# Early convolution of the first image: taps shared by two routes in every chunk, and the second pass's first weights placed over dead weights

## The chip, the cores and the metric

The kernel runs on one core of one Trainium2 chip. The time is device microseconds (us) of that core for one execution of the whole program; lower is better. All arithmetic is float32. The engines are TensorE (PE, with its weight loads as PEld), VectorE (DVE), ScalarE (ACT), GpSimd (POOL) and SyncE (SP), which here only issues DMAs. Each engine takes its instructions in the order in which the program lists them.

## What is computed

Two layers run one after the other on `x` of shape (8, 32, 32, 512): 8 images of 1024 pixels with 512 channels. The reference, cut to what matters:

```python
# layer 0: group norm, self-attention with 8 heads of 64 channels, residual
x_norm = group_norm(x, gn_scale, gn_bias)                    # 32 groups
q, k, v = split(x_norm @ w_qkv + b_qkv)
out = softmax(q k^T / 8) v                                   # per image and head, 1024 x 1024
x = x + out @ w_out + b_out

# layer 1: deformable attention
x_ln = layernorm(x, ln_g, ln_b).transpose(0, 3, 1, 2)
x_flat = x_ln.reshape(b, c, h * w).reshape(b, h * w, c)      # a reshape, not a transpose back
q = x_flat @ wq + bq
o = depthwise_conv(q.reshape(b, c, h, w), dw_w, 7x7, stride 2, padding 3)   # 16 x 16 points
offsets = conv1x1(gelu(o + dw_b), pw_w)                      # 2 numbers per point
grid = reference_points + tanh(offsets)
s = bilinear_sample(x, grid)                                 # 256 sampled rows of 512
v = k = s @ wv + bv
qh, kh, vh = heads(q @ mq_w + mq_b), heads(k @ mk_w + mk_b), heads(v @ mv_w + mv_b)
z = softmax(qh kh^T) vh @ mo_w + mo_b + x                    # 1024 queries, 256 keys
out = gelu(layernorm(z) @ mlp_w + mlp_b) + z
```

Each output of the depthwise convolution is a sum of 49 products, one for each place (u, v) of the 7x7 window. One such product and sum over a whole block of 128 channels and 256 points is called a *tap* below.

## The kernel before

**Two passes.** Pass 1 (lines 386 to 773) computes layer 0 for all images, pass 2 (lines 776 to 1195) layer 1 for all images. Between them lie two tensors in DRAM for each image: `mid`, the output of layer 0, and `hat_d`, its layer norm with scale and shift. The 512 channels are handled as four chunks of 128 partitions. The place where pass 1 ends and pass 2 begins is called the *seam*.

**Units of pass 1.** A unit is one tile of 128 queries of one pair of heads in one image. There are 32 units an image, 256 in all; where the text counts units of the last image it counts 0 to 31, and 32 and up are places after the last unit. `MovedAttention.push` writes one unit: TensorE computes the scores `sc<-k,q` (two heads, 128x1024 each), VectorE takes the row maxima `nmax`, ScalarE the exponentials `e`, and VectorE transposes them in blocks of 32x32 into `sq`. After every second unit 16 DMAs on SP move the blocks into `et`, the exponentials with keys on the partitions. Two to four units later TensorE multiplies `et` by the values (`av<-et,v`). After four units the eight sums are inverted and spread (`rs`, `rep`), turned on TensorE and copied (`inv`), and VectorE scales the result into `attT`. When an image is done, `out_steps` (lines 558 to 603) multiplies `attT` by `wout`, adds the residual tile `xr` with the bias row `bout` (which GpSimd has added to `xr` before), stores `mid`, takes the layer norm's statistics (`stats`, `mv`; GpSimd raises to the power -1/2), normalizes into `hat`, multiplies and adds the rows `lng_row` and `lnb_row` on GpSimd, and stores `hat_d`.

**The order of the work.** Whatever a unit does beside its own scores is put on a list as `at(place, step)` with a place in units, and `run_due(until)` (lines 345 to 353) writes out, in order of place, all steps due. `InOrder` keeps the written order on every engine. So a place decides the order on each engine's queue, and no scheduler changes it. A step that needs TensorE for another unit's work (the products `q`, `k` and `v` of the next pair of heads, for example, at the places in `pair_places` and, for the last pair, in `last_pair`) is called a *filler* below.

**The tail of pass 1.** For the last image the projection by `wout` comes after its last unit, at the places of `last_places` (lines 622 to 628): tiles 0 to 3, which need only the first half of the queries, from place 33.1 on, and tiles 4 to 7 from place 36 on. Its `mid` stores are issued on ScalarE's queue, its `hat_d` stores on GpSimd's; in the images before, both are on SP's.

**The early convolution** (`first_conv`, lines 630 to 715). The convolution of image 0 in pass 2 needs only `hat_d` of image 0, which is there long before. So it is computed in pass 1, among the units of the last image, by chunks of output channels 0 to 3. `fetch` loads `wq` into four buffers, its bias row, and the tap weights `dww_x`. For each chunk `operand` loads two halves of `hat_d`, `fill` multiplies them by `wq` on TensorE (two matmul groups), and `fill_end` adds the bias row and writes the result into an image with a border of zeros, the *pad* (`conv_pad`). Then come 49 taps, in one of two forms (`conv_tap`):

- alone: one VectorE instruction multiplies the strided pad by the tap weight and adds it to the accumulator;
- shared: ScalarE writes the product into one half of a small buffer `part_x` (two halves, used in turn), and GpSimd adds it to the accumulator.

All 49 taps of chunks 0 and 1 are shared; they use one pad, which lies with the bias row in a buffer of the tag `xT`. All 98 taps of chunks 2 and 3 are alone; their two pads and their accumulators lie in a tile of the tag `wqkv`, 24,576 bytes on each partition, which takes the place of the layer's `w_qkv` weights and so can be filled only when the last product with these is done. Of the 98, ten are placed from unit 27.9 on, sixteen with the eight `wout` tiles (two for each), and 72 after all tiles. `store` sends the finished sums to `o_first` in DRAM by GpSimd's queue.

**The start of pass 2** (`prep`, lines 836 to 873). SP's queue issues `wq_r` (the weight `wq` again), `wv`, `mk_w`, seven small vectors, and later `mv_w` and `mq_w`. TensorE turns `wq_r` and `wv` (16 transposes each), and then multiplies them by `mk_w`, `mv_w` and `mq_w` (`product`, four groups each), so that later each of keys, values and queries takes one product. `add_cols` makes the bias columns. `points(0)` (lines 943 to 951) stands after the first of the four `mq_w` products: it loads `o_first` (as `o`, on SP), applies gelu on ScalarE, computes the offsets on TensorE (`mm<-pww,o`), tanh, the corner indices on VectorE, gathers rows of `mid` with indirect DMAs on GpSimd's queue, and sums them with their weights into `smp`. After `prep` come the four key steps and two value steps of image 0 and the first units of pass 2. Small loads for the convolution (`load_conv`: `dwb`, `dww`, two for `pww`) and the rows `bq_row`, `bo_row`, `bm_row` are issued in `load_late`, behind the `mv_w` bias column.

**Pools of pass 2** (line 783). A pool's buffers take the addresses that pass 1 leaves, in the order in which the pools are opened, and a load into a buffer waits until all that lay at its addresses in pass 1 has been read. Here the order is

```python
cv, late, late2, first, cvhat, raw, wp
```

where `first` holds `wq_r`, `raw` the raw weights `wv`, `mk_w`, `mv_w`, `mq_w` in two buffers of 8,192 bytes a partition, and `cv` the small tiles of the convolution and two pads.

Of the kernel before, what the change touches and what calls it, by code (L numbers as in the profile page):

```python
# [9 lines left out]
F32 = mybir.dt.float32  # L10
# [220 lines left out]
def attention_then_deformable_attention(  # L231
# [137 lines left out]
    def conv_tap(acc, pad, dww, cb, u, v, part=None):  # L369

        tap = dww[:, cb, u * KS + v : u * KS + v + 1]
        src = pad[:, ds(u, G, 2), ds(v, G, 2)]
        acc = acc.rearrange("p (i j) -> p i j", j=G)
        first = u == 0 and v == 0
# [11 lines left out]
    with ExitStack() as l0:  # L386
# [171 lines left out]
        def out_steps(b, attT, places, last=False):  # L558
# [22 lines left out]
            def summed(t):  # L581
# [3 lines left out]
                stats = work.tile([P, 6], F32, tag="stats", name="stats1", bufs=2)  # L585
# [44 lines left out]
        def first_conv(n):  # L630
# [3 lines left out]
            room = {"pad": {}, "o": {}}  # L634

            def fetch():
# [3 lines left out]
                rest = work.tile([P, NC, QB], F32, tag="xT", name="rest_x", bufs=NX_T)  # L640
                rest = rest.rearrange("p c q -> p (c q)")
                room["bq"] = rest[:, 0:C]
# [3 lines left out]
                pad = rest[:, ds(C, PADH * PADW)]  # L646
                nc.gpsimd.memset(pad, 0.0)
                pad = pad.rearrange("p (i j) -> p i j", j=PADW)
                part = work.tile([P, C], F32, tag="hat", name="part_x", bufs=3)
                o = work.tile([P, C], F32, tag="hat", name="o_x", bufs=3)  # L650
                room["part"] = part
                for cb in range(2):
                    room["pad"][cb], room["o"][cb] = pad, o[:, ts(cb, NS)]

            def fetch2():
                pads = wp.tile([P, NC, 3 * C], F32, tag="wqkv", name="pads_x")
                o = pads[:, 2, :]
                for i in range(2):
                    pad = pads[:, i, 0 : PADH * PADW]
                    nc.gpsimd.memset(pad, 0.0)  # L660
                    room["pad"][2 + i] = pad.rearrange("p (i j) -> p i j", j=PADW)
                    room["o"][2 + i] = o[:, ts(i, NS)]
# [16 lines left out]
            def fill_end(cb, par):  # L679
                conv_pad(room["pad"][cb], room["ps", cb, par], room["bq"], par)  # L680

            def tap(cb, i, part):
                conv_tap(
                    room["o"][cb], room["pad"][cb], room["dww"], cb, i // KS, i % KS,
                    (lambda: room["part"][:, ts(i % 2, NS)]) if part else None,
                )

            def store(cb):
                nc.gpsimd.dma_start(o_first[:, cb, :], room["o"][cb])

            at(n + 10.5, fetch)
            at(n + 24, fetch2)
            taps = KS * KS
            for cb, start in enumerate((12.2, 22.5, 25.2, 27.2)):
                at(n + start - 1.6, lambda cb=cb: operand(cb))
                for par in range(2):
                    at(n + start + par, lambda cb=cb, par=par: fill(cb, par))
                    at(n + start + par + 0.65, lambda cb=cb, par=par: fill_end(cb, par))
                if cb < 2:
                    for i in range(taps):  # L700
                        at(n + start + 1.7 + 0.18 * i, lambda cb=cb, i=i: tap(cb, i, True))
                    at(n + start + 10.7, lambda cb=cb: store(cb))


            for j in range(2 * taps):
                cb, i = divmod(j, taps)
                if j < 10:
                    place = n + 27.9 + 0.4 * j
                elif j < 26:
                    place = last_places(n + per, (j - 10) // 2)[2] + 0.02  # L710
                else:
                    place = n + per + 12
                at(place, lambda cb=cb + 2, i=i: tap(cb, i, False))
# [515 lines left out]
```

## Time and profile before

| | us |
|---|---|
| three timed runs | 3788.79, 3792.98, 3794.7 (median 3792.98) |
| the profiled execution's own time | 3789.67 |
| span of that execution on the core | 3788.0 |
| TensorE busy | 3578.3 (94%) |
| VectorE busy | 2789.1 (74%) |
| ScalarE busy | 1529.3 (40%) |
| GpSimd busy | 750.6 (20%) |

Every time of a trace is in microseconds from the start of the span. The mean granted clock of TensorE over the span is 0.975 of full speed. The seam lies near 2070 us: pass 1 takes some 55% of the span. Nearly all instructions are recorded by one helper, so all carry one line number (L53), and groups are told apart by their tiles: `mm<-wout,attT` is a matmul that reads `wout` and `attT` and writes a tile `mm`; a trailing `_x` marks tiles of the early convolution, and numbers of buffers are left out. In the rows, `PE mm L53 <- DMA wq_r: 9.0, 1, 9.0` says that TensorE stood idle before an `mm` instruction 9.0 us in all, in one wait, longest 9.0, and that what ended the wait was the landing of the load of `wq_r`; `x16 [9.01 <-...]` in a timeline is a group of 16 instructions and the idle time before it. `SPq` is the issuing queue of SP.

### The profile page before, as it was taken

Reading aid. Unit: us, or ns where it says so; the run is one execution under the profiler, and the core shown is the slowest. Engines: PE = TensorE matmul, PEld = TensorE weight load, DVE = VectorE, ACT = ScalarE, POOL = GpSimd, SP = SyncE. Lnnn points to the kernel's source line nnn. Section 1 sums busy time; section 2 is a strip of 40 time slices with the busy share of each in tenths; the row PEclk is TensorE's granted clock in tenths of the full one; section 3 lists DMA queues with packets and bytes.
Section 4 is the critical chain, followed back from the end, with each engine's and each line's share of the span. In section 5 each row is a group of like instructions: output and inputs, shape, how many; then the busy total and the mean of one; then the engine's idle time right before and its main releaser. Section 6 shows DMA issues by size and latency. Waiting matters only on the chain.

```text
span 3788.0 us, 46075 instructions
## 1 busy us (share of the span) xinstructions
PE 3578.3 (94%) x16152; PEld 1868.9 (49%) x16152; DVE 2789.1 (74%) x4264; ACT 1529.3 (40%) x3218; POOL 750.6 (20%) x838
## 2 busy tenths in 40 slices
PE   8999999999999999999998787999999999999997
PEld 4554554545545455455453434454545454544543
DVE  5678777776777777867766569898988888888333
ACT  3443443433434434344364123343434343444443
POOL 0003012020030120301346201121121212121212
PEclk9999999999999999999999898999999999999999
DMA  5667666665666666655755501021111111110100
GB/s 154 155 158 188 164 168 170 162 184 153 162 189 159 170 168 163 188 155 150 199 143 143 176 1 67 34 71 41 67 45 56 56 56 56 56 56 34 59 23 31
DMA packets 235350, 438.23 MB, mean 116 GB/s; under 512 B 49296, under 2 KB 53392, under 8 KB 232176
## 3 DMA queue, kind: packets, MB, share of 16 engines
q1 hardware_dynamic: 212528, 363.08, 35.4%
q0 software_dynamic: 21440, 70.11, 5.8%
q8 instruction: 129, 2.11, 0.2%
q10 hardware_dynamic: 1152, 2.10, 0.2%
q14 instruction: 101, 0.83, 0.1%
HBM read 115.84 MB, written 50.86 MB: 44 GB/s over the span
## 4 chain that ended last, share of the span: by engine, by line
PE 69%; DVE 20%; issue 6%; DMA 1%; ACT 1%; POOL 1%; SPq 0%; DVEq 0%; POOLq 0%; ACTq 0%
PE mm L53 42%; PE sc L53 15%; PE av L53 13%; DVE o L53 10%; DVE nmax L53 3%; DVE stats L53 1%; DVE sq L53 1%; DVE pad L53 1%; POOL mv L53 1%; ACT e L53 1%; DVE z L53 1%; DVE zn L53 1%; DVE attH L53 1%; DVE mv L53 1%; DMA row<-mid,ii 0%
## 5 line engine op out<-in xcount | busy, mean ns | idle before, releaser
L53 ACT ACTIVATE e<-sc,nmax 128x1024 f32<-128x1024 f32 (+1 forms) x1024 | 804.6, 799 | 901.8 <-DVE nmax L53 901.3
L53 DVE TENSOR_REDUCE nmax<-sc 128x1 f32<-128x1024 f32 (+1 forms) x640 | 753.2, 1219 | 481.5 <-PE sc L53 480.3
L53 DVE SCALAR_TENSOR_TENSOR o<-pad,dww,o 128x256 f32<-128x256 f32 x1344 | 721.3, 537 | 44.1
L53 DVE STREAM_TRANSPOSE sq<-e 128x1024 f32<-128x1024 f32 x512 | 608.1, 1226 | 50.8 <-ACT e L53 49.5
L53 PE MATMUL sc<-k,q 64*128 64x512 f32 x2048 | 527.3, 618 | 13.5 <-ACT q L53 6.2
L53 PE MATMUL av<-et,v 128*64 128x256 f32 x4096 | 504.2, 389 | 16.3 <-DMA et<-sq 9.4
L53 PE MATMUL mm<-xT,wqkv 128*128 128x512 f32 x1024 | 471.5, 604 | 2.6 <-issue 2.6
L53 PEld LDWEIGHTS av<-et,v 128*64 128x64 f32 x4096 | 276.0, 138 | 322.9 <-issue 177.2
L53 POOL TENSOR_TENSOR mv<-mv,minus_half 128x1 f32<-128x1 f32 x128 | 74.3, 581 | 1396.3 <-DVE mv L53 1334.1
L53 PEld LDWEIGHTS sc<-k,q 64*128 64x128 f32 x2048 | 181.6, 186 | 276.2 <-issue 229.8
L53 PEld LDWEIGHTS mm<-xT,wqkv 128*128 128x128 f32 x1024 | 185.9, 191 | 226.8 <-issue 219.7
L53 ACT COPY et<-mm 128x512 f32<-128x512 f32 x256 | 140.7, 593 | 317.6 <-PE mm L53 317.4
L53 PE MATMUL mm<-wqkv,xT 128*128 128x128 f32 x2048 | 244.5, 278 | 0.0
L53 PEld LDWEIGHTS mm<-wqkv,xT 128*128 128x128 f32 x2048 | 233.8, 192 | 19.9 <-issue 19.9
L53 PE MATMUL mm<-wm,zT 128*128 128x512 f32 x512 | 240.4, 613 | 2.9 <-ACT zT L53 2.9
L53 PE MATMUL mm<-hat_h,wqq 128*128 128x512 f32 x512 | 236.7, 605 | 0.0
L53 PE MATMUL mm<-wo,attH 128*128 128x512 f32 x512 | 231.4, 595 | 3.1 <-DVE attH L53 3.1
L53 PE MATMUL mm<-wout,attT 128*128 128x512 f32 x512 | 233.7, 601 | 0.0
L53 ACT ACTIVATION_READ_ACCUMULATOR e<-sc,nmax 128x1 f32 x1024 | 209.2, 204 | 0.0
L53 PE MATMUL mm<-wq_r,hat 128*128 128x512 f32 x448 | 203.8, 598 | 0.2 <-ACT et L53 0.2
L53 PE MATMUL mm<-ident,e 128*128 128x128 f32 x1024 | 152.6, 293 | 26.7 <-DVE z L53 11.4
L53 PEld LDWEIGHTS mm<-hat_h,wqq 128*128 128x128 f32 x512 | 92.1, 189 | 143.0 <-issue 131.6
(153 smaller groups left out, 3629.5 us busy)
## 6 DMA issues: line engine op xcount, KB each, us to landing
et<-sq SPq DMA_DIRECT2D x2048, 128.0 KB, 2.7
xr<-in_x_dram POOLq DMA_DIRECT2D x64, 256.0 KB, 3.7
hat_h<-hat_d SPq DMA_DIRECT2D x16, 1024.0 KB, 5.3
xr<-mid SPq DMA_DIRECT2D x64, 256.0 KB, 3.1
out_dram<-res POOLq DMA_DIRECT2D x64, 256.0 KB, 2.3
x<-in_x_dram POOLq DMA_DIRECT2D x60, 256.0 KB, 3.8
mid<-xr SPq DMA_DIRECT2D x56, 256.0 KB, 2.9
hat_d<-hat SPq DMA_DIRECT2D x56, 256.0 KB, 2.9
```

The source lines that it names most:

```text
L53: return self.tc.keep_in_program_order(op(*args, **kwargs))
```

## The change

It has three parts.

1. *The taps of every chunk are split between the two routes.* `conv_tap` takes a running tap number and a flag for the first of an accumulator. Taps 0 to `shared[cb]`-1 of chunk `cb` are shared (29, 29, 29, 11), the rest alone (20, 20, 20, 38), into the second half of the chunk's `o_x` buffer; `store` adds the two halves on VectorE before the DMA. The pads come from two buffers of the tag `xT` instead of the tile over `w_qkv` (chunks 0, 1 and 3 use the one, chunk 2 the other), the accumulators from the tags `hat` and `x`. The fills move to the places in `fills`, the taps start at `begins` with a shared tap every 0.18 and an alone tap every 0.265 units. Chunk 3's first 24 taps of both kinds come with the `wout` tiles, three for each, and the last 14 alone after all of them. `last_pair` moves four of the last pair's six fillers: 21.3 to 22.3, 22.3 to 23.3, 23.3 to 24.3 and 23.6 to 25.3. The tail's `stats` get a tag of their own.
2. *Another order of pools in pass 2.* `wq_r` and the two raw-weight buffers come first and so lie where `w_qkv` lay, 24,576 bytes a partition; the two pads and the rows `bo_row` and `bm_row` get a pool `padp` of their own.
3. *Two moves in* `prep`. `load_conv` goes from `load_late` to the place before the load of `mv_w`, and `points(0)` from after the first `mq_w` product to after the second `mk_w` product, six groups and two bias columns earlier.

```diff
@@ -366,12 +366,12 @@
         )
-    def conv_tap(acc, pad, dww, cb, u, v, part=None):
-
+    def conv_tap(acc, pad, dww, cb, i, first, part=None):
+
+        u, v = divmod(i, KS)
         tap = dww[:, cb, u * KS + v : u * KS + v + 1]
...
         acc = acc.rearrange("p (i j) -> p i j", j=G)
-        first = u == 0 and v == 0
         if part is not None:
@@ -582,7 +582,7 @@
                 to_mid.dma_start(dst[:, t, :], xr)
-                stats = work.tile([P, 6], F32, tag="stats", name="stats1", bufs=2)
+                stats = work.tile([P, 6], F32, tag="stats1", name="stats1", bufs=2)
                 mv = room["mv", t] = work.tile([P, 3], F32, tag="mv1", name="mv1", bufs=3)
@@ -631,35 +631,25 @@
-            room = {"pad": {}, "o": {}}
+            room = {}
             def fetch():
...
                     nc.gpsimd.dma_start(room["w"][c], by_chunk(wq)[:, c, :])
-                rest = work.tile([P, NC, QB], F32, tag="xT", name="rest_x", bufs=NX_T)
-                rest = rest.rearrange("p c q -> p (c q)")
-                room["bq"] = rest[:, 0:C]
+                rest = padded(0)
+                room["bq"] = rest[:, ds(PADH * PADW, C)]
                 nc.gpsimd.dma_start(room["bq"], bq.partition_broadcast(P))
...
                 nc.gpsimd.dma_start(room["dww"], dw_w.rearrange("(c p) a u v -> p c (a u v)", p=P))
-                pad = rest[:, ds(C, PADH * PADW)]
+
+            def padded(i):
+                rest = work.tile([P, NC, QB], F32, tag="xT", name="rest_x", bufs=NX_T)
+                rest = rest.rearrange("p c q -> p (c q)")
+                pad = rest[:, 0 : PADH * PADW]
                 nc.gpsimd.memset(pad, 0.0)
-                pad = pad.rearrange("p (i j) -> p i j", j=PADW)
-                part = work.tile([P, C], F32, tag="hat", name="part_x", bufs=3)
-                o = work.tile([P, C], F32, tag="hat", name="o_x", bufs=3)
-                room["part"] = part
-                for cb in range(2):
-                    room["pad"][cb], room["o"][cb] = pad, o[:, ts(cb, NS)]
-
-            def fetch2():
-                pads = wp.tile([P, NC, 3 * C], F32, tag="wqkv", name="pads_x")
-                o = pads[:, 2, :]
-                for i in range(2):
-                    pad = pads[:, i, 0 : PADH * PADW]
-                    nc.gpsimd.memset(pad, 0.0)
-                    room["pad"][2 + i] = pad.rearrange("p (i j) -> p i j", j=PADW)
-                    room["o"][2 + i] = o[:, ts(i, NS)]
+                room["pad", i] = pad.rearrange("p (i j) -> p i j", j=PADW)
+                return rest
             def operand(cb):
@@ -677,42 +667,44 @@
             def fill_end(cb, par):
-                conv_pad(room["pad"][cb], room["ps", cb, par], room["bq"], par)
-
-            def tap(cb, i, part):
+                conv_pad(room["pad", pad_of[cb]], room["ps", cb, par], room["bq"], par)
+
+            def tap(cb, i, alone):
+                if i == 0:
+                    tag = dict(tag="hat", bufs=3) if cb < NC - 1 else dict(tag="x", bufs=NX)
+                    room["o", cb] = work.tile([P, C], F32, name="o_x", **tag)
+                    if cb in (0, NC - 1):
+                        room["part"] = work.tile([P, C], F32, name="part_x", **tag)
                 conv_tap(
-                    room["o"][cb], room["pad"][cb], room["dww"], cb, i // KS, i % KS,
-                    (lambda: room["part"][:, ts(i % 2, NS)]) if part else None,
+                    room["o", cb][:, ts(int(alone), NS)], room["pad", pad_of[cb]], room["dww"], cb, i,
+                    i in (0, shared[cb]), None if alone else lambda: room["part"][:, ts(i % 2, NS)],
                 )
             def store(cb):
-                nc.gpsimd.dma_start(o_first[:, cb, :], room["o"][cb])
-
+                o = room["o", cb]
+                nc.vector.tensor_tensor(o[:, 0:NS], o[:, 0:NS], o[:, ts(1, NS)], ALU.add)
+                nc.gpsimd.dma_start(o_first[:, cb, :], o[:, 0:NS])
+
+            pad_of = (0, 0, 1, 0)
+            shared = (29, 29, 29, 11)
+            fills = ((12.35, 13.35), (20.6, 21.3), (26.3, 27.3), (28.3, 29.3))
+            begins = (14.05, 22.05, 28.0, 33.05)
             at(n + 10.5, fetch)
-            at(n + 24, fetch2)
-            taps = KS * KS
-            for cb, start in enumerate((12.2, 22.5, 25.2, 27.2)):
-                at(n + start - 1.6, lambda cb=cb: operand(cb))
+            at(n + 22.4, lambda: padded(1))
+            for cb in range(NC):
+                at(n + fills[cb][0] - 1.6, lambda cb=cb: operand(cb))
                 for par in range(2):
-                    at(n + start + par, lambda cb=cb, par=par: fill(cb, par))
-                    at(n + start + par + 0.65, lambda cb=cb, par=par: fill_end(cb, par))
-                if cb < 2:
-                    for i in range(taps):
-                        at(n + start + 1.7 + 0.18 * i, lambda cb=cb, i=i: tap(cb, i, True))
-                    at(n + start + 10.7, lambda cb=cb: store(cb))
-
-
-            for j in range(2 * taps):
-                cb, i = divmod(j, taps)
-                if j < 10:
-                    place = n + 27.9 + 0.4 * j
-                elif j < 26:
-                    place = last_places(n + per, (j - 10) // 2)[2] + 0.02
-                else:
-                    place = n + per + 12
-                at(place, lambda cb=cb + 2, i=i: tap(cb, i, False))
-            at(n + per + 13, lambda: store(2))
-            at(n + per + 13, lambda: store(3))
+                    at(n + fills[cb][par], lambda cb=cb, par=par: fill(cb, par))
+                    at(n + int(fills[cb][par]) + 0.95, lambda cb=cb, par=par: fill_end(cb, par))
+                for i in range(KS * KS):
+                    alone, j = i >= shared[cb], i - shared[cb] * (i >= shared[cb])
+                    place = n + begins[cb] + (0.265 if alone else 0.18) * j
+                    if cb == NC - 1:
+
+                        place = last_places(n + per, j // 3 % NT)[2] + 0.02
+                        place = place if j < 24 else n + per + 12
+                    at(place, lambda cb=cb, i=i, alone=alone: tap(cb, i, alone))
+                at(n + begins[cb] + (5.1 if cb < NC - 1 else 20), lambda cb=cb: store(cb))
         per = NHP * NT
@@ -725,7 +717,7 @@
         ]
-        last_pair = (19.3, 20.3, 21.3, 22.3, 23.3, 23.6)
+        last_pair = (19.3, 20.3, 22.3, 23.3, 24.3, 25.3)
         norm_places = [
@@ -780,8 +772,8 @@
             return l1.enter_context(tc.tile_pool(name=name, bufs=bufs, reuse_waits="tile"))
-        cv, late, late2, first, cvhat, raw, wp = (
-            pool(n) for n in ("cv", "late", "late2", "first", "cvhat", "raw", "w2")
+        first, raw, padp, cv, late, cvhat, late2, wp = (
+            pool(n) for n in ("first", "raw", "padp", "cv", "late", "cvhat", "late2", "w2")
         )
@@ -826,7 +818,7 @@
         nc.vector.tensor_scalar(refs, refs, -1.0, None, ALU.add)
-        pads = [cv.tile([P, PADH, PADW], F32, tag=f"pad{i}", name=f"pad{i}") for i in range(PADS)]
+        pads = [padp.tile([P, PADH, PADW], F32, tag=f"pad{i}", name=f"pad{i}") for i in range(PADS)]
         for pad in pads:
@@ -854,6 +846,7 @@
             load_small()
+            load_conv()
             for m in range(NC):
@@ -864,7 +857,7 @@
                     product(dst, k, raws[name], i)
-                    if name == "mq" and i == 0:
+                    if name == "mk" and i == 1:
                         points(0)
@@ -895,7 +888,7 @@
                 conv_out(b)
-            conv_tap(room[b, "o"][:, cb, :], pads[cb % PADS], dww, cb, i // KS, i % KS)
+            conv_tap(room[b, "o"][:, cb, :], pads[cb % PADS], dww, cb, i, i == 0)
         def conv_gelu(b):
@@ -1157,9 +1150,8 @@
             wm = load_w(late2, mlp_w, "wm")
-            bo_row = load_row(late, mo_b, "bo_row")
-            bm_row = load_row(late2, mlp_b, "bm_row")
-            load_conv()
+            bo_row = load_row(padp, mo_b, "bo_row")
+            bm_row = load_row(padp, mlp_b, "bm_row")
         def rows():
...
```

## The prediction

> **What bounds the kernel now.** I read the page first: whole-span shares, then the chain. TensorE is busy 94% and carries 69% of the chain, so only places where TensorE waits, or does nothing useful, can pay.
>
> ```profile
> PE 3578.3 (94%) x16152; PEld 1868.9 (49%) x16152; DVE 2789.1 (74%) x4264; ACT 1529.3 (40%) x3218; POOL 750.6 (20%) x838
> ...
> PE 69%; DVE 20%; issue 6%; DMA 1%; ACT 1%; POOL 1%; SPq 0%; DVEq 0%; POOLq 0%; ACTq 0%
> ```
>
> The change lies around the seam of the two passes, so next the waits of TensorE from 2030 to 2200 us (in all, times, longest), and TensorE's timeline there (start, us, group, count, idle before it and what ended that).
>
> ```profile
> PE av L53 <- DMA et<-sq: 9.4, 1, 9.4
> PE mm L53 <- DMA wq_r<-in_L_conv_wq_dram: 9.0, 1, 9.0
> PE mm L53 <- DVE smp L53: 8.8, 1, 8.8
> PE mm L53 <- ACT o L53: 2.5, 1, 2.5
> ```
>
> ```profile
> 2062.26 6.59 PE L53 MATMUL av<-et,v 128*64 128x256 f32 x32 [9.40 <-DMA et<-sq]
> 2070.47 13.90 PE L53 MATMUL mm<-wout,attT 128*128 128x512 f32 x32
> 2093.38 3.65 PE L53 MATMUL mm<-ident,wq_r 128*128 128x128 f32 x16 [9.01 <-DMA wq_r<-in_L_conv_wq_dram]
> 2143.01 3.55 PE L53 MATMUL mm<-pww,o 128*128 128x2 f32 x16 [2.50 <-ACT o L53]
> 2181.24 7.03 PE L53 MATMUL mm<-wvv,smp 128*128 128x512 f32 x16
> ```
>
> Four holes, 29.7 us. The second ends on a weight load, the third on the gather of `points(0)`; those two, 17.8 us, are what the change goes for. The start of the value steps, 2181.24, is my finish line: from there the second pass is the same in both programs, and VectorE, which bounds its first images, is idle 23.64 us up to 2195.23, so a shift there moves all that follows.
>
> Then who sets the seam. These are rows of GpSimd's timeline, of VectorE's, and two waits of SP's queue:
>
> ```profile
> 2039.75 3.23 POOL L53 DMA_DIRECT2D xr<-in_x_dram  x6
> 2047.88 5.30 POOL L53 TENSOR_TENSOR xr<-xr,bout 128x512 f32<-128x512 f32 x4 [1.46 <-DMA xr<-in_x_dram]
> 2053.14 3.92 POOL L53 TENSOR_TENSOR o_x<-part_x,o_x 128x256 f32<-128x256 f32 x5
> ```
>
> ```profile
> 2092.09 15.01 DVE L53 SCALAR_TENSOR_TENSOR pads_x<-pads_x,dww_x 128x256 f32<-128x256 f32 x23
> 2107.40 24.96 DVE L53 SCALAR_TENSOR_TENSOR pads_x<-pads_x,dww_x 128x256 f32<-128x256 f32 x48
> ```
>
> ```profile
> SPq L53 <- DVE mv L53: 27.8, 1, 27.8
> SPq L53 <- DMA mid<-xr: 15.0, 1, 15.0
> ```
>
> GpSimd's queue is the hidden bound: the last `et` pieces stand on SP behind the first two `mid` stores (15.0), those stand on ScalarE behind taps that wait for GpSimd's adds, and these stand behind the six `xr` adds. VectorE's 72 late taps end at 2132.4, which is why `points` cannot come sooner.
>
> Last, busy time in single units (PE, PEld, DVE, ACT, POOL): the cover for new taps.
>
> ```profile
> 1914.81:1922.23 7.42, 7.42 (x33) 3.18 (x32) 4.73 (x4) 5.20 (x10) 3.82 (x6) 1.00 0.30 78
> 2006.68:2014.10 7.42, 7.42 (x33) 3.18 (x32) 6.57 (x8) 5.48 (x11) 4.47 (x7) 1.00 0.72 180
> ```
>
> **Part by part.** *Taps in the units.* Chunks 0 to 2 now put 20 taps each on VectorE, at 3 or 4 a unit. A tap repeats every 0.52 us (24.96/48). Units 22 to 29 then hold on VectorE 8 x 4.73, 28 taps 14.6, four pads at 0.69, two `rs`/`rep` pairs at 1.07, two `attT` at 0.65, one new sum near 0.4: 59.0 us, against TensorE's 60.4 (7.42 a unit, 7.56 with values, 7.82 with `rep`). Units 14 to 19: 42.7 against 45.6. `nmax` may come some 2.0 us late before the next scores wait (5.4 us of other matmuls, less 1.2 of `nmax`, 2.2 of exponentials). So it fits, barely: cost 0, cover 1.4 + 2.0 us. A tap beside GpSimd's adds: below, 0.485 alone; above, 0.83, the longest beside such an add; three there average 0.60 (0.51, 0.47, 0.83), which I take as the nearest: same tap, same adds. Cover over 28 taps is 0.12 each: it holds to 0.64 from tap to tap, and 0.60 with the gap is 0.635.
> [...]
>
> *Matmuls moved.* Nothing is added on TensorE; fillers go from units 22 and 23 into 24 and 29. Unit 24 was empty (0.73 idle and 1.2 of waits inside its scores): -1.95. But `k` now ends right before unit 24's scores: +0.8, as `sc<-k,q` waited 0.78 for `q` in unit 15. The sums at units 19 and 27 wait for GpSimd's last add and hold `sq`: 2.5 us, hidden by `et` slack of about 2.5, +0.3. So unit 30's scores start at 2017.1 (2017.9 less 0.85). Then VectorE has no hole: scores 1.9, lag 0.7, `nmax` 2.4, four taps with `sq`, `rs` and `rep` 5.2, `nmax` 2.4, an exponential 1.2: `inv` at 2030.9 instead of 2033.88. Six adds follow in 5.9, as before: GpSimd's `xr` loads begin at 2036.8, 3.0 sooner. Its loads and adds take 13.4 (2039.75 to 2053.14): 2050.2.
>
> *The tail of pass 1.* Now worse. GpSimd has 6 adds instead of 5 (0.78 each) before the sum of chunk 2, and VectorE's sum stands ahead of `xr` of tile 0, which stood free before. From 2050.2: adds 4.7, sum 0.4, `xr` 0.7, statistics 1.1, 3 taps 1.4, `xr` of tile 1 0.7: its `mid` store goes out at 2059.2 (before about 2056.2), so the last `et` lands near 2065, +3. Behind it GpSimd carries 8 of chunk 3's adds between the tiles' `mv` and `hat`. From 2050.2: 14 adds 11.0, four `mv` 2.4, two `hat` pairs 5.3, three stores 2.5, waits for VectorE 2.5: 23.7; VectorE's last `hat`, `rs` and `rep` 2.2: 2076.1, against 2069.98: +6.1. The same wout follows: TensorE done at 2090.5 (before 2084.4).
>
> *Weights.* `wq_r`, `wv`, `mk` wait only for the last pieces of `et` and a `mid` store, near 2072: landing in 5.7 to 11.9 they are there by 2084. The 9.0 us hole goes; next late is the third transpose, for `xr` of tile 7 (about 2094). Six more groups 5.1, a copy 0.6, two products 6.9: TensorE is at `points` near 2107.
>
> *Points earlier.* GpSimd's chain ends 54.7 after 2050.2 (before 44.7 after 2053.14; eleven more adds, 8.6, and 1.4 of waits). VectorE's last 14 taps start at 2097.8; six squeeze in beside it, 8 run free, 4.2: 2108.2; sum 0.4, store 2.2 (2132.66 to 2134.86), `o` load: 3.6 as before, or 9.2 if the 1 MB `mv` load now just ahead (5.6) delays it fully; I take 4.2. Table 1.28, first gelu 0.43, offsets 3.55: 2120.3. So TensorE waits about 10 us here, where it waited 2.5: what the weight load gave is half given back. SP's four small convolution loads now stand ahead of `mv` and `o`, and the first of them waits for the last taps: `mv` goes out near 2109 instead of 2101.5, needed at 2131; `mq` behind `o` and mk's end, lands at 2137, needed at 2148: hidden by 17 us of products, and a late one would cost its lateness one for one.
>
> *Rest.* Two mk products 6.9, three bias columns 3.5 each, eight products 27.6: 45.0. The granted clock was 0.55 to 0.69 for some 10 us after holes like this (2090 to 2100, 2160 to 2170): a cost between 0 and 5, I take 2.5. TensorE reaches the key steps at 2167.8; the gather, 21.6 us (2150.0 to 2171.6), is done near 2146, so no hole. Key steps 4 x 1.81 at full clock: value steps at 2175.0 against 2181.24.
>
> **The sum:** -6.2 us. The profiled execution took 3789.67 (span 3788.0, 1.7 around it): 3783.5. It stands 3.3 under the median of the three, 3792.98; for the median I say 3787.
>
> **Rivals.**
> *The convolution is there in time.* Every microsecond that GpSimd's tail is shorter is one gained, up to the 10 that TensorE waits. For it: `xr` landed in 7.0 us, 3.8 is its median elsewhere (-3); the clock's 2.5; my GpSimd waits of 2 may vanish. 3776 to 3784, say 3780. Against it: GpSimd's order holds eleven more adds, whatever their luck.
> *Slower: VectorE and GpSimd in each other's way.* Place: units 14 to 29 and the tail's taps. At 0.86 a tap (0.83 and the gap) instead of 0.52, units 22 to 29 overrun their cover by 6.2 us and 14 to 19 by 1.8, which takes the 6.2 back and 1.8 more; in the tail, where taps beside 1.26 us operations took 1.2 to 1.66, 24 of them can put up to 15 of their 20 us on the chain. 3795 to 3810, say 3802. It decides from 0.64 us from tap to tap. Against it: most of a unit's taps follow `nmax`, while ScalarE does exponentials and feeds GpSimd nothing.
> *No change.* The hole at `points` equals what was won: another 5 us, as if `o` landed late by its upper bound. 3790 to 3797.
>
> **Chances.** Forecast 0.45 (3782 to 3791, its own range), in time 0.24, no change 0.15, slower 0.16. This kernel's runs tell about 0.2% from no change, 7.6 us: below 3785.4 lie all of the second and 0.17 of the first: 0.41; above 3800.6 two thirds of the slower case: 0.11; same 0.48. Range 3778 to 3798: a quarter of the second case (0.06) and four fifths of the slower one (0.13) stay out.
>
> **What will show it.** No `wq_r` wait; a wait of about 10 us of `pww` matmuls on ScalarE's `o`; no wait on `smp`; `rep` of the last group near 2076; units of 7.4 to 7.9 us up to 29, with VectorE near 7.3. Wrong if `sc` waits for exponentials in units 14 to 29, if GpSimd passes the last `hat` store before 2098 or after 2110, or if `o` lands before 2107.

## The result: 0.3% slower

The changed kernel takes 3804.16 us (median of 8 runs, 3798.71 to 3807.73), the kernel before 3791.43 (8 runs): a ratio of 1.0034, 95% interval 1.0023 to 1.0045. A later set of runs beside the experiments gave 3800.57 against 3792.74, 1.0022 (1.0008 to 1.0036). So 8 to 13 us were lost where 4 to 6 were forecast as gained. The profiled execution took 3807.61 us, its span is 3805.9.

Whole spans are a poor ruler here: from the value steps to the end, where all kernels here do the same work, the profiles of this study take between 1603 and 1616 us (the last section shows what goes with it). So I compare landmarks in the seam, counted from the start of unit 10's scores in the last image, which comes before everything that was changed (1849.84 us in the profile before, 1850.31 after). In those terms the value steps, the finish line of the forecast, come 11.9 us later than before (331.40 and 343.29).

The page after, first part and chain, shows no other bound than before:

```profile
PE 3587.8 (94%) x16152; PEld 1871.5 (49%) x16152; DVE 2789.8 (73%) x4268; ACT 1529.1 (40%) x3218; POOL 749.0 (20%) x835
...
PE 69%; DVE 20%; issue 6%; POOL 2%; ACT 2%; DMA 1%; SPq 0%; DVEq 0%; POOLq 0%; ACTq 0%
```

The waits of TensorE from 2030 to 2200 us after (us in all, times, longest) say what replaced what:

```profile
PE mm L53 <- ACT o L53: 14.6, 1, 14.6
PE mm L53 <- DVE rep L53: 7.7, 1, 7.7
PE mm L53 <- DVE xr L53: 7.1, 2, 4.5
PE av L53 <- DVE attT L53: 6.2, 1, 6.2
```

The waits for `wq_r` (9.0) and for `smp` (8.8) are gone, and that for `et` fell from 9.4 to 3.4. In their place stand 14.6 us before the offsets (2.5 before) and some 21 us of waits for VectorE in the tail (2.5 before). TensorE's timeline after (start, us, group, count, idle before it and what ended that):

```profile
2058.00 5.84 PE L53 MATMUL mm<-wout,attT 128*128 128x512 f32 x8 [4.54 <-DVE xr L53]
...
2078.60 1.12 PE L53 MATMUL mm<-ident,rep 128*128 128x128 f32 x4 [7.66 <-DVE rep L53]
2079.51 15.55 PE L53 MATMUL mm<-wout,attT 128*128 128x512 f32 x32
...
2098.50 0.66 PE L53 MATMUL mm<-ident,wq_r 128*128 128x128 f32 x4 [2.57 <-DVE xr L53]
...
2125.14 3.57 PE L53 MATMUL mm<-pww,o 128*128 128x2 f32 x16 [14.64 <-ACT o L53]
2128.57 9.82 PE L53 MATMUL mm<-raw,wT 128*128 128x512 f32 x16
2138.23 4.43 PE L53 MATMUL mm<-bv_c,raw 128*128 128x1 f32 x32
2142.51 16.54 PE L53 MATMUL mm<-raw,wT 128*128 128x512 f32 x32
...
2184.16 9.60 PE L53 MATMUL mm<-smp,wvk 128*128 128x256 f32 x32
2193.60 7.03 PE L53 MATMUL mm<-wvv,smp 128*128 128x512 f32 x16
```

Two things are to be seen. Up to the end of `wout` the tail is 10.2 us later than before (counted from unit 10): 8.1 of them are there at `rep`, and `wout` itself takes 15.55 us instead of 13.90. And behind the offsets the same matmuls last longer: 16 matmuls `mm<-raw,wT` take 9.82 us and 32 take 16.54, with no wait between them, where 32 took 13.97 in the trace before:

```profile
2100.53 13.97 PE L53 MATMUL mm<-raw,wT 128*128 128x512 f32 x32 [0.78 <-ACT wT L53]
```

The forecast's own landmarks against the profile after (the offsets' 2116.7 is its 2120.3 less their 3.55 us):

| | forecast | after |
|---|---|---|
| GpSimd's `xr` loads begin | 2036.8 | 2039.67 |
| its `xr` adds end | 2050.2 | 2052.19 |
| `mid` store of tile 1 | 2059.2 | 2061.38 |
| `rep` of the last group | 2076.1 | 2078.60 |
| `wout` done | 2090.5 | 2095.06 |
| TensorE at `points` | 2107 | 2110.50 |
| last 14 taps begin | 2097.8 | 2103.89 |
| offsets begin | 2116.7 | 2125.14 |
| key steps | 2167.8 | 2184.16 |
| value steps | 2175.0 | 2193.60 |

Two rows of VectorE's timeline after show where its queue stood; in brackets the idle time before. The first is unit 27, the second the tail:

```profile
2004.22 0.42 DVE L53 TENSOR_TENSOR o_x<-o_x 128x256 f32<-128x256 f32 x1 [2.65 <-POOL o_x L53]
...
2056.92 0.42 DVE L53 TENSOR_TENSOR o_x<-o_x 128x256 f32<-128x256 f32 x1 [16.39 <-POOL o_x L53]
...
2103.89 10.30 DVE L53 SCALAR_TENSOR_TENSOR o_x<-rest_x,dww_x,o_x 128x256 f32<-128x256 f32 x14
```

Both are the new sum of a chunk's two halves, waiting for GpSimd's last add. In the tail it held VectorE for 16.39 us with `xr` of tile 0 behind it, which TensorE then waited for.

### The profile page after: what moved, and what is told of

It is laid out like the page before. It is cut to its first block, busy times and chain, and to the rows that moved or that the text cites. A ratio compares the mean times of both kernels' runs of the same rounds, so it can differ in the third digit from the quotient of the medians.

```text
span 3805.9 us, 46077 instructions
## 1 busy us (share of the span) xinstructions
PE 3587.8 (94%) x16152; PEld 1871.5 (49%) x16152; DVE 2789.8 (73%) x4268; ACT 1529.1 (40%) x3218; POOL 749.0 (20%) x835
## 4 chain that ended last, share of the span: by engine, by line
PE 69%; DVE 20%; issue 6%; POOL 2%; ACT 2%; DMA 1%; SPq 0%; DVEq 0%; POOLq 0%; ACTq 0%
PE mm L53 42%; PE sc L53 14%; PE av L53 12%; DVE o L53 10%; DVE nmax L53 3%; DVE stats L53 1%; DVE sq L53 1%; ACT e L53 1%; DVE pad L53 1%; POOL mv L53 1%; DVE z L53 1%; DVE zn L53 1%; DVE attH L53 1%; DVE mv L53 1%; DVE o_x L53 0%
```

## The experiments

Each ran beside the kernel before; ratios are to that, with 95% intervals. "Value steps" are differences to the kernel before, counted from unit 10, where the changed kernel has +11.9 and, profiled once more, +11.7 us.

**points(0) back behind the first mq_w product** (e1).

```diff
-                    if name == "mk" and i == 1:
+                    if name == "mq" and i == 0:
                         points(0)
```

> The changed kernel with points(0) back behind the first mq_w product; taps, pools and load_conv stay as changed. Theory (the earlier points(0) puts TensorE before a convolution that is not ready): the 14.6 us wait for o goes, TensorE reaches the offsets near 2141.6 us after 31.1 us of products and bias columns, and waits some 11 us for the samples (28.6 us from the start of the offsets to smp in the trace of before); value steps near 2178 to 2180, against 2193.6 in the changed kernel: 14 to 16 us less, 3788 to 3790 us, about the time of before. Rival (the loss is in the taps of units and tail, the place of points(0) only moves a wait from o to smp): 0 to 5 us less, 3799 to 3804.

3797.53 us, 1.0016 (1.0007 to 1.0025); value steps +7.2. The wait for `o` fell to 2.5 us, and a wait for the samples came back:

```profile
PE mm L53 <- DVE smp L53: 9.1, 1, 9.1
```

The gain, 4.7 us at the value steps, is a third of what the theory expected, and the time is nearer to the rival's: the offsets came at 2150.4 instead of 2141.6, since products and bias columns ahead of them were slower than reckoned. With the changed first pass TensorE waits at either place.

**points(0) cut in two** (e2): the load of `o` stays, gelu, offsets and gather come behind the second `mv_w` product.

```diff
                     if name == "mk" and i == 1:
-                        points(0)
+                        points_load(0)
+                    if name == "mv" and i == 1:
+                        points(0)
...
```

> The changed kernel with points(0) cut in two: the load of o stays behind the second mk_w product, gelu, offsets and gather come behind the second mv_w product, 17.4 us of TensorE's work later. Theory (the 14.6 us wait is the loss, and there is a place without a wait on either side): o is ready at 2125, TensorE is there near 2128, waits at most 2.5 us for table and gelu, and has 27.7 us of products left to cover the gather's 25 us; value steps at 2168 to 2171, 22 to 25 us before the changed kernel: 3779 to 3783 us, faster than before by 8 to 12. Rival (the granted clock falls in the same way after the bias columns whatever waits): half of it, 3787 to 3791.

3785.23 us, 0.9982 (0.9974 to 0.9991): faster than before, and 15 to 19 us under the changed kernel's two medians, between theory and rival. Value steps -2.3. The wait for `o` is 2.5 us, that for `smp` gone:

```profile
2134.64 3.57 PE L53 MATMUL mm<-pww,o 128*128 128x2 f32 x16 [2.50 <-ACT o L53]
```

From the offsets to the value steps it took 45.0 us, where the theory's own landmarks leave 37.5 to 40.5 (2168 to 2171 less 2130.5, which is 2128 and a wait of 2.5). The place of `points(0)` alone turned the sign; taps, pools and loads are those of the changed kernel.

**The sums later** (e3): behind `sq` and `attT` in the units, behind tile 1's sum of `xr` in the tail.

```diff
-                at(n + begins[cb] + (5.1 if cb < NC - 1 else 20), lambda cb=cb: store(cb))
+                at(n + (19.95, 27.95, 33.16, 53.05)[cb], lambda cb=cb: store(cb))
```

> The changed kernel with the sum of the two halves of a chunk (VectorE, waits for GpSimd's last add) moved behind what it held up: behind sq and attT in units 19 and 27, and behind the sums of xr of tiles 0 and 1 in the tail. Theory (the sums hold VectorE's queue): the two attT waits of TensorE in the units (0.97 and 1.70 us) go, the wait for xr of tile 0 (4.5 us) goes, the first mid stores go out near 2056 instead of 2058 and 2061.4, rep of the last group is 3 to 5 us sooner; the whole 3 to 6 us less, 3798 to 3801. Rival (the length of GpSimd's queue in the tail decides, with 11 adds among the tiles): TensorE's waits only move, rep within 1.5 us of 2078.6, the whole within 2 us of the changed kernel.

3798.25 us, 1.0009 (0.9998 to 1.0019); value steps +7.5. Unit 30 starts 2.8 us sooner than in the changed kernel (167.39 against 170.18 after unit 10), which is the two `attT` waits of 0.97 and 1.70 us; `rep` comes 5.5 us sooner, a little more than the theory had. Of that 4.7 us are left at the offsets, for which TensorE now waits 16.3 us, and 4.4 at the value steps. The time is the theory's.

**The first pass alone** (e4): first pass of the changed kernel, second pass of the one before.

```diff
-        first, raw, padp, cv, late, cvhat, late2, wp = (
+        cv, late, late2, first, cvhat, raw, wp = (
...
-            load_conv()
...
-                    if name == "mk" and i == 1:
+                    if name == "mq" and i == 0:
                         points(0)
...
```

> The changed kernel's first pass (tap split, pads, fillers, tail) with the second pass of before: old order of pools, load_conv late, points(0) behind the first mq_w product. Theory (the split of the taps costs some 9 to 11 us up to the end of wout, whatever stands behind it): wq_r is again waited for, some 10 us after wout, o is not, smp is; value steps near 2190, 9 to 10 us behind before: 3799 to 3802 us. Rival (the split itself is free and the second pass's part loses the time): within 3 us of before, 3789 to 3794.

3796.18 us, 1.0010 (1.0001 to 1.0019); value steps +7.7, between theory and rival in time. `wout` ends 10.0 us later than before, as the theory said, and `smp` is waited for (8.5 us). But there is no wait for `wq_r`: its load goes out at 2074.81 and is there in time with the old order of pools too. So the hole of 9.0 us that the forecast credited to the new pools goes with the new first pass alone. Which of its edits frees `wq_r` wasn't tried. In the trace before, SP held that load 27.8 us for VectorE's `mv`, which reads `stats`; the new tag of the tail's `stats` would fit, but this is argued.

**TensorE kept busy in the wait** (e5): four product groups, thrown away, ahead of the offsets.

```diff
...
-        def points(b):
+        def points(b, thrown_away):
+            for i in range(4):
+                thrown_away(i)
             conv_out(b)
...
```

> The changed kernel with four product groups whose results are thrown away put on TensorE just before the offsets of points(0), 13.7 us of work into its wait of 14.6 us for o; nothing else moves. Theory (the wait costs twice: idle, and then half a granted clock from 2123 to 2134 us and after, since TensorE stood idle): offsets start within 1 us of where they did, the half-clock stretch of 20.5 us from 2113.6 is gone, the products behind run at full clock, value steps 4 to 6 us sooner: 3797 to 3801. Rival (the clock falls for other reasons, the bias columns for one, or comes back at once): within 2 us of the changed kernel, 3802 to 3807.

3796.53 us, 1.0014 (1.0006 to 1.0023), which is 4 to 8 us under the changed kernel's two medians. Yet the profiled execution, one of the longest of its twelve (3804.65), doesn't show the mechanism: the offsets start at the same time from unit 10 (274.4 and 274.8), the half-clock stretch of 20.5 us at 2113.6 is gone, but another of 6.8 us begins 1.8 us behind the start of the offsets, and from there to the value steps it takes 68.0 us instead of 68.5. TensorE's rows of e5:

```profile
2122.43 2.95 PE L53 MATMUL mm<-pww,o 128*128 128x2 f32 x16 [1.28 <-ACT o L53]
2125.24 10.01 PE L53 MATMUL mm<-raw,wT 128*128 128x512 f32 x16
```

The idle time alone is thus not what slows the products behind. It is inconclusive on the theory's 4 to 6 us; e11 shows where the clock went.

**e2 and e3 together** (e6).

> The cut points(0) of e2 and the later sums of e3 together. Theory (the two losses are apart: VectorE held by the sums up to rep, TensorE before o afterwards): the 4 to 6 us of e3 come on top of e2, value steps near 2174 to 2176, 3779 to 3782. Rival (behind the cut points(0) the next thing to end late is the convolution again or the mv_w load, which the sums do not move): within 2 us of e2, 3783 to 3787.

3782.20 us, 0.9978 (0.9970 to 0.9987); value steps -12.5. In the seam this is 10.2 us on top of e2's: 6.0 up to the offsets and 4.3 behind them, where the same work took 40.7 us instead of 45.0. In the median it makes 3.0 us, between theory and rival.

**Chunk 3 without GpSimd** (e7): e6, and all 49 taps on VectorE, 14 of them before tile 0's sum.

```diff
-            shared = (29, 29, 29, 11)
+            shared = (29, 29, 29, 0)
...
-                        place = last_places(n + per, j // 3 % NT)[2] + 0.02
-                        place = place if j < 24 else n + per + 12
+                        place = last_places(n + per, (j - 14) // 3 % NT)[2] + 0.02
+                        place = place if j < 38 else n + per + 12
+                        place = place if j >= 14 else n + per + 0.9
...
```

> As e6, and chunk 3's eleven shared taps also done by VectorE alone: 14 of its 49 taps before the sum of tile 0 (VectorE was idle there for 16.4 us in the changed kernel), 24 with the tiles as before, 11 after them; no add of chunk 3 on GpSimd. Theory (the eleven adds, 8.6 us, stand in GpSimd's queue before the last hat of tiles 0 to 3 and so hold rep): rep 3 to 6 us before that of e6, wout ends near 2084 to 2087, value steps 2168 to 2172, 3773 to 3778. Rival (VectorE's taps beside hat operations, not GpSimd's adds, set that time): rep within 1.5 us of e6 and the whole within 2 us of it.

3776.22 us (five runs), 0.9961 (0.9948 to 0.9974); value steps -9.4. The median is the theory's, 6 us under e6's, though the value steps of its profile come 3.1 us later than e6's. `rep` moved by 0.75 us only (222.5 against 223.2 in e6), as the rival said. But this is no clean test of the eleven adds in GpSimd's queue. The 14 early taps cost VectorE 0.92 us each, mostly beside GpSimd's 128x512 adds, and put tile 0's `xr` 6.6 us later than in e6 (from unit 10); from there to `rep` it takes 7.4 us less (22.4 against 29.8). What the adds alone held is not shown. VectorE's row of e6, then those of e7 (its 14 taps and the `xr` of tile 0 behind them):

```profile
2040.60 0.69 DVE L53 TENSOR_TENSOR xr<-mm,xr 128x512 f32<-128x512 f32 x1 [6.04 <-PE mm L53]
```

```profile
2037.26 12.91 DVE L53 SCALAR_TENSOR_TENSOR o_x<-rest_x,dww_x,o_x 128x256 f32<-128x256 f32 x14
2050.10 0.68 DVE L53 TENSOR_TENSOR xr<-mm,xr 128x512 f32<-128x512 f32 x1
```

**No tap among the tiles** (e8): as e7, with all 49 taps after them (lines marked - are the changed kernel's).

```diff
-                        place = last_places(n + per, j // 3 % NT)[2] + 0.02
-                        place = place if j < 24 else n + per + 12
+                        place = n + per + 12
```

> As e7, but all 49 taps of chunk 3 after the tiles, so that no tap stands among them. Rival to e7's theory first: if VectorE's taps among the tiles hold rep, it comes 3 us or more before that of e7. Theory: rep within 2 us of e7, since GpSimd's queue sets it; 49 taps of 0.49 us, 24 us, then start near 2097 and end at 2121, o lands near 2129 and TensorE waits some 5 us for it: 3 to 6 us more than e7, 3777 to 3783.

3789.91 us, 0.9998 (0.9989 to 1.0007); value steps -2.8. `rep` comes 6.3 us sooner than in e7 and 4.0 sooner than before. The profile puts this on the 14 taps ahead of the tiles: `xr` of tile 0 comes 6.9 us sooner than in e7, and from there to `rep` takes 23.0 us against 22.4. The time was then lost elsewhere, to a wait that no theory had, first TensorE's wait, then SP's rows:

```profile
PE mm L53 <- DMA raw<-in_L_conv_mv_w_dram: 20.3, 1, 20.3
```

```profile
2116.94 0.37 SPq L53 DMA_DIRECT2D dwb<-in_L_conv_dw_b_dram  x1
...
2119.06 0.45 SPq L53 DMA_DIRECT2D raw<-in_L_conv_mv_w_dram  x1
```

`dwb` waits 30.2 us for the last tap, and `mv_w` stands behind it on SP.

**load_conv behind mv_w** (e9): as e8, and

```diff
             load_small()
-            load_conv()
...
             fetch(mv_w, "mv")
+            load_conv()
```

> As e8, with load_conv moved from ahead of the load of mv_w to behind it; nothing else. Theory (in e8 the load of mv_w stood on SP's queue for 30 us behind dwb, whose place in memory the last taps still use; that, not the taps, cost e8 its gain): the 20.3 us wait for mv_w goes, TensorE comes to the offsets near 2111 and waits some 14 us for o, offsets near 2125 instead of 2137.4, value steps 10 to 13 us sooner than in e8: 3777 to 3781 us. Rival (mv_w is late for its buffer, or the wait only moves to o in full): within 3 us of e8, 3787 to 3793.

3783.94 us, 0.9977 (0.9964 to 0.9991), against 0.9998 in e8; value steps -5.9. The wait for `mv_w` is gone, the offsets come 9.1 us sooner (from unit 10), and TensorE waits 10.8 us for `o`. The mechanism is the theory's and the time lies between theory and rival. The profile's value steps gained 3.1 instead of 10 to 13, since the same work behind the offsets took 47.9 us up to the value steps, 41.9 in e8: the first 16 products 9.94 us instead of 8.94, the next 32 products 16.66 instead of 13.98.

**The parts that helped, together** (e10): e9 with seven taps before tile 0 and the second part of `points(0)` behind the fourth `mv_w` product.

```diff
-                        place = n + per + 12
+                        place = n + per + (0.9 if j < 7 else 12)
...
-                    if name == "mv" and i == 1:
+                    if name == "mv" and i == 3:
                         points(0)
```

> As e9, with seven of chunk 3's taps before the sum of tile 0, where e8 showed VectorE idle and GpSimd not yet adding, the other 42 after the tiles, and gelu, offsets and gather of points(0) behind the fourth mv_w product. Theory (rep then comes as early as in e8, o some 4 us sooner, and the products of mv_w fill TensorE's wait): rep as in e8 within 1.5 us, offsets near 2121 to 2124 with a wait under 5 us, the samples the last to come, value steps near 2159 to 2163: 3765 to 3771 us, faster than both kernels. Rival (the seven taps push the sum of tile 0 as the fourteen in e7 did, and the samples are late): rep 2 us or more later than in e8, 3772 to 3778.

3771.16 us (five runs, 3770.21 to 3774.27), 0.9952 (0.9938 to 0.9965): faster than both kernels. Value steps -16.7. `rep` is 2.3 us later than in e8, which is the rival's number, but only 0.5 later than in e9, whose tail is that of e8; the wait before the offsets is the 2.5 us of table and gelu, and the samples were not waited for:

```profile
2067.01 1.12 PE L53 MATMUL mm<-ident,rep 128*128 128x128 f32 x4 [2.48 <-DVE rep L53]
...
2125.12 3.57 PE L53 MATMUL mm<-pww,o 128*128 128x2 f32 x16 [2.50 <-ACT o L53]
...
2163.21 7.03 PE L53 MATMUL mm<-wvv,smp 128*128 128x512 f32 x16
```

**Without the bias columns** (e11).

```diff
-                add_cols(bias, raws[name], b_in, on_scalar=True)
```

> The changed kernel without the three bias columns of prep (96 matmuls of 128x1), so keys, values and queries lack their biases from bv and bq. Their own time is 13.8 us in the changed kernel's trace, 10.5 at full clock. Theory (such matmuls keep TensorE so little busy that the granted clock falls to a half behind them, as after all three in the changed kernel): from the offsets to the value steps 45 to 50 us instead of 68.5, so 18 to 23 us less; the whole 3781 to 3786. Rival (the half clock there has other reasons): 54 to 58 us, 10 to 14 less; 3790 to 3794.

3781.65 us, 0.9976 (0.9967 to 0.9985), 18.9 under the changed kernel in the same stretch. From the offsets to the value steps 47.8 us instead of 68.5: the theory's number, with the same 14.8 us wait ahead of it. The windows of the changed kernel and then of e11 (us, busy of PE, PEld, DVE, ACT, POOL, granted clock, DMA share, GB/s) show the clock:

```profile
2130.00:2145.00 15.00, 15.00 (x50) 8.79 (x49) 6.52 (x24) 1.89 (x6) 8.42 (x8) 0.73 0.45 138
2145.00:2160.00 15.00, 15.00 (x41) 7.06 (x39) 0.94 (x2) 2.34 (x4) 0.00 (x0) 0.91 0.76 264
2160.00:2175.00 15.00, 15.00 (x45) 8.53 (x45) 0.00 (x0) 1.89 (x6) 0.00 (x0) 0.77 0.21 71
```

```profile
2130.00:2145.00 15.00, 15.00 (x34) 6.54 (x34) 3.25 (x5) 2.34 (x4) 7.75 (x8) 0.95 0.75 239
2145.00:2160.00 15.00, 15.00 (x36) 6.65 (x35) 2.25 (x3) 2.34 (x4) 0.00 (x0) 1.00 0.63 233
2160.00:2172.00 12.00, 12.00 (x44) 8.13 (x44) 0.00 (x0) 3.07 (x6) 0.00 (x0) 1.00 0.62 242
```

TensorE is busy throughout in both. With columns the clock is granted by half for 6.8 us at each of the three, from 2.3 to 2.6 us behind its start on; without them it stays full from 2131.6 on, past the start of the value steps (2170.50). The products behind the offsets are then one row of e11:

```profile
2126.14 37.27 PE L53 MATMUL mm<-raw,wT 128*128 128x512 f32 x80
```

At the 10.9 us that the columns took in the trace before (3 x 3.63), 9.8 of the 20.7 us are the clock's.

**The changed kernel again** (e12).

> The changed kernel as it is, beside e9 to e11 and the kernel before in the same stretch of runs. Theory (the spread over its runs comes from where the clock's steps of 3.4 us fall, the median from the program): median within 3 us of 3804, the profile's landmarks within 3 us from the start of the units on, and the half-clock stretches in other places. Rival (the loss depends on the stretch of runs): median under 3798.

3800.57 us, 1.0022 (1.0008 to 1.0036): 3.6 under the first median, a little more than the theory allowed, and its eleven runs span 3791.67 to 3810.51. The landmarks repeat (unit 30 to 0.01 us, value steps to 0.2), and so do the half-clock stretches behind all three columns: they lie in the same places, not in others as I had expected, and what stands behind the columns takes as long to within 0.14 us (16.68, 16.51 and 9.72 us, in the first profile 16.54, 16.37 and 9.60).

## Why the prediction was wrong

It forecast -6.2 us at the value steps; the profile has +11.9.

*Taps in the units: right on average, wrong on one term.* Three taps behind `nmax` took 1.51 to 1.71 us, under the 0.64 from tap to tap that was the limit, and most units kept 7.4 to 7.9 us. "The sums at units 19 and 27 ... hidden by `et` slack of about 2.5, +0.3": they cost 2.8, shown by e3. Each held `sq`, `attT` and so TensorE.

*"`inv` at 2030.9 instead of 2033.88"* came at 2033.60, since unit 30 was late: from its scores to `inv` it took 13.1 us, less than the 13.8 of the sum, and with the sums moved (e3) `inv` comes 2.8 us sooner. Of the 3.0 us gained for GpSimd's `xr` loads 0.5 were there, counted from unit 10.

*The tail: right in sign and about right in size (+6.1 forecast for `rep`, +8.1 measured).* The 2.0 us more came in with the late unit 30; from GpSimd's last `xr` add to `rep` it took 26.4 us, 25.9 were forecast. The step put the tail on GpSimd's queue, with eight more adds. VectorE's queue was as full: from 2056.92 to `rep` it waits once, 1.24 us for GpSimd's `mv`. The sums waiting on VectorE cost 5.5, the 2.8 of the units among them (e3). Leaving out GpSimd's eleven adds and VectorE's taps among the tiles together gains 5.3 to 7.1 more (e9 and e8 against e6); how that divides is not shown.

*Weights: right that the hole goes* and that the third transpose, waiting for `xr` of tile 7, is late next (2.57 us). But the new pools weren't needed for it (e4).

*Points earlier: right place, sized too small.* "TensorE waits about 10 us here": 14.6. The last 14 taps began 6.1 us later than forecast. The forecast left 21.7 us from `rep` to them, about the 22.1 of the trace before, where each `wout` tile has two taps; with three it took 25.3, and the taps of tiles 4 to 7 took 9.2 us instead of 5.3. The 14 taps ran 0.74 us each, as forecast, and `o` took 5.55 us from issue to gelu's table load, with the 1 MB load of `mv_w` issued 1.3 us ahead of it; the trial value 4.2 was too low. The wait was in the forecast, its remedy wasn't: e2 shows 15 to 19 us between this place and one four product groups and a bias column later. SP's small loads ahead of `mv_w` were hidden as the text said, but only behind that wait; e8 brought them out at 20.3 us.

*Rest: this is the step that failed most.* "A cost between 0 and 5, I take 2.5" for the clock. From offsets to key steps it took 59.0 us instead of 51.1, and the key steps 9.44 instead of 7.2: 10.1 us more. e11 puts 9.8 on the bias columns. The forecast looked for low clock only behind holes, where e11 loses 2.4 (37.27 us for 80 matmuls; 34.9 at the full clock of the trace before, where 32 take 13.97), much as its 2.5 had it; behind the bias columns it put nothing. In the trace before, the first column was followed by no such stretch, the second by 3.4 us and the third by the hole for `smp`, so their price was hidden there.

*The sum.* 8.4 us too early at the offsets and 10.1 behind them, by the table above. Counted from unit 10 the first part is 8.0: 2.0 up to `rep`, 3.6 to the last taps, 2.3 in storing and loading `o`. None of the forecast's signs of being wrong came, and none of them looked behind the offsets. Of the rivals, "slower" had the number (3802), in part by luck, since it has only part of the mechanism (taps in the tail, not in the units) and no clock; "no change" had the hole at `points`, with 5 us more in it. The range ended at 3798 because I gave the slower case 0.16 and cut most of it off; with a clock term of up to 12.6 us, which is what it came to and which the trace didn't exclude, it would have reached the result.

## What to carry to other kernels

A step moved earlier gains nothing by itself: find when its input is ready and when its result is needed, and put it where TensorE's other work covers both sides; a load can be issued early and its use come later. A step that waits for another engine belongs on an in-order queue behind all that doesn't need it; here the sums held work for 3 to 16 us, and one small load held another for 20. And differences of a few tenths of a per cent need landmarks in the trace, counted from a point ahead of the change, since the clock moved whole times by as much (e12: 3791.67 us in the run with a mean granted clock of 0.978, 3810.51 in one with 0.971).

## What the runs showed of the hardware that I had not expected

- Half clock (a granted clock of 0.50) came behind matmuls with no idle time around them in the profile: 32 of 128x1, 4.4 to 4.8 us in the changed kernel, each with a stretch of 6.8 us from 2.3 to 2.6 us behind its start on. It didn't come each time: no such stretch comes behind the first column of the kernel before, nor behind the second of e6 and e8, and the 32 products behind each of these take 13.98 us. All stretches of half clock in the traces before and after, but for the last, which ends with the trace, last a multiple of 3.41 us (3.4, 6.8, 10.2, 13.7 and 20.5). The last three stretches in the seam of the changed kernel have no wait ahead of them, and without the columns they are gone (e11). What in the columns brings them is not shown: that they keep TensorE little busy was the theory of e11, and the profile has it busy throughout.
- In the changed kernel they repeat: stretches start at 2140.9, 2161.3 and 2181.8, 20.48 us or six steps of 3.413 apart, and e5, e9 and e12 have the same spacing (their columns start 20.66 or 20.67 us apart). A round of four products and a column takes 20.7 us once it is slowed, close to that, so the next column falls at nearly the same place of a step. That this keeps the pattern going is argued, not shown.
- The same holds in the second pass: from the scores of its unit 16 to those of unit 24 it takes 194.5 or 194.6 us with 6.8 us of half clock (before, e7, e8, e10) or 196.4 to 196.5 with 10.2 (after, e3, e5, e9), and 194.56 is 57 steps of 3.413. Neighbouring images mostly repeat it (all five at 194.6 or less in e10, four of five above 196 in e9), which goes, in part, with second passes of the same work that differ by up to 13 us from the value steps on.
- A VectorE tap took 0.485 us alone, 0.74 on average in the changed kernel's last 14 and 0.92 mostly beside GpSimd's 128x512 adds (e7): moved into VectorE's idle time, it wasn't free.
